# x times W1_r of 44 node blocks computed ahead, kept in HBM, and loaded in place of x

## The chip, the core and the metric

The kernel runs on one core of a Trainium2 chip. A core has five engines with queues of their own: TensorE (PE, matrix products into PSUM; PEld is its weight load), VectorE (DVE), ScalarE (ACT), GpSimd (POOL, which here issues the indirect loads that gather rows) and SyncE (SP, which here issues nearly all other transfers). Each engine works off its instructions in order and waits on semaphores for the others. The metric is the device time of one execution in microseconds (us), lower is better. Three executions of the kernel before took 3142.34, 3150.2 and 3154.97 us; the median is 3150.2 us.

## What is computed

Two graph convolutions, a linear layer, a residual and a layer norm, over 12500 nodes of 256 features and 200000 edges sorted by destination:

```python
def _sage_conv(x, src, dst, W_l, b_l, W_r):
    msgs = x[src]
    agg = segment_sum(msgs, dst, num_segments=N_NODES)
    deg = segment_sum(ones, dst, num_segments=N_NODES)
    mean = agg / maximum(deg, 1.0)[:, None]
    return mean @ W_l + b_l + x @ W_r
h = relu(_sage_conv(x, src, dst, W1_l, b1, W1_r))
h = relu(_sage_conv(h, src, dst, W2_l, b2, W2_r))
out = layernorm(x + h @ W3 + b3)
```

The destinations are crowded at low node numbers. All numbers are fp32.

## The kernel before

Nodes are cut into 98 blocks (`NB`) of 128. The sums over edges are made in two ways, and both run beside each other through each of the two layers.

Blocks 0 to 11 (six groups of 256 nodes in the first layer, `HG1 = 6`, `DN = 256`) have so many edges that a dense count matrix is cheaper: `count` (L887) builds, tile by tile of 128 edges, the number of edges from every source to every destination of the group. DVE makes 0/1 masks (`pick` L912, `low` and `aft` L902), PE multiplies them into `count_ps` (L946, L950), and ACT writes them to SBUF (L952). `product` (L820) then multiplies the counts with x, split in three bf16 parts (L842), block by block, and `degrees` (L964) sums the counts (L970). The next group is counted while the last one is multiplied.

All other blocks are gathered. A round (`Gathers.step`) is four indirect loads of 128 rows each on POOL (L277) into one of four buffers `got`, and eight small PE products (L289, `part_ps`); every one or two rounds, further products (L305, L311) put the sums in order, and DVE adds them to a ring `sums` (L315, L319). The first layer has 257 rounds. A round's buffer is free for the gather of four rounds later once its L289 products have run.

When a block's sums are complete, `first_block` (L1127) makes its layer output in three pieces: it loads the block's x (`load_rows`, L1067) and yields; it turns x by two PE transposes (L1073) and an ACT copy (L1075) and yields; `sage` (L1098) multiplies turned x by W1_r (two L1102 products, which show as four rows) and the sums by W1_l (L1104), DVE adds the bias (L1111) and the scaled sums (L1112), ACT takes the maximum with 0 (L1157), and SP stores the block (L1160, L1163).

PE and POOL are in an order written out by the program itself. `layer` (L627) takes one round after another, with up to three pieces of waiting blocks, and then fills the round with pieces of the dense work (count, product, degrees, given by `stages_1`) until the largest of its cost sums over PE, DVE and ACT reaches 5.05. When the dense work is used up, a round is only gathers and block pieces. In the last 8 rounds the dense work must be done; then come the rest of the blocks. Stage 0 of `stages_1` counts the first group with no product beside it; its count begins after the setup.

The setup (L321 to L581) loads the edge lists and turns them into tables: `columns` (L398) is a ping-pong of DVE, which makes a column of keys (L517), PE, which transposes it (L404), and DVE, which clamps it into a table (L407). Twelve gather rounds (`early_round`, L476) stand between. At its end DVE runs tests on the edge lists (L531 to L579) that decide at the very end of the program whether a second method has to run (it does not here). The memory pools of the counts are opened after the setup's pool closes and lie on its memory.

Of the kernel before, what the change touches and what calls it, by code (L numbers as in the profile page):

```python
# [25 lines left out]
P = 128  # L26
# [23 lines left out]
def by_runs(  # L50
# [66 lines left out]
    def room(t):  # L117
        return ROOMS[t // 32]
# [15 lines left out]
    h2_d = dram.tile([P, NB, 2, D], F32, name="h2_d")  # L134
    ORDER = [*reversed(range(HG1)), *range(HG1, HG)]
# [106 lines left out]

    def left_after(g):

        return NB if g == len(groups) - 1 else min(max(int(at_least(groups[g + 1][0]) // P), 0), NB)
# [75 lines left out]
    with tc.tile_pool(name="setup", bufs=1) as su, \  # L321
            tc.tile_pool(name="setup_ps", bufs=2, space=PSUM) as su_ps:
# [159 lines left out]


# [8 lines left out]
        columns(low, (0, HC), low_t, "low", 0, 0, HT)  # L492
        high = su.tile([P, HC, P], F32, name="high")
# [14 lines left out]
        for g in ORDER:  # L508
# [6 lines left out]
            for i, (to, name, since) in enumerate(((key_t[g], "key", lows[g]), (after_t[g], "aft", after_from[g]))):  # L515
# [3 lines left out]
                columns(key, (c0, c1), to, name, c0, since, highs[g])  # L519

# [5 lines left out]

        early_round()
# [8 lines left out]
                                       op1=OP.mult, accum_out=test())  # L536
        early_round()
# [39 lines left out]
        for a, b in zip([FIRST - 1] + ends, ends):  # L577
# [3 lines left out]
                                       accum_out=test(1))  # L581


    def weight(w, name, tag, queue=nc.scalar):
        t = consts.tile([P, NC, w.shape[1]], F32, name=name, tag=tag)
        queue.dma_start(t, w.rearrange("(c p) f -> p c f", p=P))
        return t

    w1l_sb, w1r_sb = weight(w1l, "w1l_sb", "wl"), weight(w1r, "w1r_sb", "wr")
# [17 lines left out]
    def held(g):  # L607

        return counts[ORDER.index(g) % 2]

# [487 lines left out]
    def sage(own_t, b, agg, since, wl, wr, bias):  # L1098

        ps = block_bank()  # L1100
        for c in range(NC):
            nc.tensor.matmul(ps[:, 1], lhsT=own_t[:, c], rhs=wr[:, c], start=c == 0, stop=c == NC - 1)  # L1102
# [8 lines left out]
        nc.vector.tensor_add(own, ps[:, 1], bias)  # L1111
# [15 lines left out]
    def first_block(b, agg=None):  # L1127
        x_sb = load_rows(x, N, b, "x_sb")
# [16 lines left out]
        ps = turned()  # L1145
        known = of_ring and b in upto
        if known:
            summed(ps)
        x_t = transposed(x_sb, ps, "own_t")
        yield 0.5, 0.0, 0.37  # L1150
# [5 lines left out]
        h = sage(x_t, b, agg, since, w1l_sb, w1r_sb, biases[:, 0])  # L1156
# [7 lines left out]
        yield 1.75, 1.65, 1.1  # L1164
# [430 lines left out]
```

## Time and profile before

| what | us |
|---|---|
| median of 3 runs (lowest, highest) | 3150.2 (3142.34, 3154.97) |
| the profiled execution, its own time | 3149.7 |
| its span on the core's trace | 3147.4 |
| setup, to the first count product | 0 to 97 |
| stage 0 (first count) | 97 to 205 |
| rest of the first layer | 205 to 1688 |
| second layer | 1688 to 3147 |

Busy time and "x" counts are per engine; "PEclk" is the share of the full TensorE clock that the throttle granted. A row of the chain of waits is a start, a length, and the instruction (engine, tile, line, number of rows) that the end of the program hung on in that time. "remote" or "another core or an unknown queue" stands where a semaphore came without an instruction that the trace could name for it; this program runs on one core.

### The profile page before, as it was taken

Reading aid. Unit: us, or ns where it says so; the run is one execution under the profiler, and the core shown is the slowest. Engines: PE = TensorE matmul, PEld = TensorE weight load, DVE = VectorE, ACT = ScalarE, POOL = GpSimd, SP = SyncE. Lnnn points to the kernel's source line nnn. Section 1 sums busy time; section 2 is a strip of 40 time slices with the busy share of each in tenths; the row PEclk is TensorE's granted clock in tenths of the full one; section 3 lists DMA queues with packets and bytes.
Section 4 is the critical chain, followed back from the end, with each engine's and each line's share of the span. In section 5 each row is a group of like instructions: output and inputs, shape, how many; then the busy total and the mean of one; then the engine's idle time right before and its main releaser. Section 6 shows DMA issues by size and latency. Waiting matters only on the chain.

```text
span 3147.4 us, 51161 instructions
## 1 busy us (share of the span) xinstructions
PE 2509.2 (80%) x17028; PEld 1731.9 (55%) x17028; DVE 1422.9 (45%) x4363; ACT 1345.2 (43%) x2435; POOL 1887.7 (60%) x1946
## 2 busy tenths in 40 slices
PE   3578888888888888888876878887877888887876
PEld 1245556566655555556653555555655556665654
DVE  5566644344444476654232124334543344343344
ACT  0476644445455411463122444555554445433322
POOL 6666756556566566665654665666655666666653
PEclk8799989899899898999987998999989899998989
DMA  4359887786776555656755876777767777676643
GB/s 118 87 181 316 275 266 230 221 267 217 242 243 207 160 176 176 186 168 203 251 160 176 266 236 209 253 243 223 234 217 225 229 227 234 209 223 193 203 139 93
DMA packets 392876, 659.49 MB, mean 210 GB/s; under 512 B 61055, under 2 KB 217757, under 8 KB 392605
## 3 DMA queue, kind: packets, MB, share of 16 engines
q1 hardware_dynamic: 295315, 401.44, 40.0%
q0 software_dynamic: 92928, 253.88, 26.5%
q8 instruction: 140, 2.29, 0.3%
q10 hardware_dynamic: 4362, 0.80, 0.2%
q14 instruction: 131, 1.07, 0.1%
HBM read 559.60 MB, written 96.29 MB: 208 GB/s over the span
## 4 chain that ended last, share of the span: by engine, by line
PE 69%; issue 9%; DVE 6%; ACT 5%; another core or an unknown queue 5%; DMA 3%; POOL 0%; DVEq 0%; ACTq 0%; SPq 0%; POOLq 0%
PE dense_ps L842 11%; PE part_ps L289 9%; PE count_ps L946 9%; PE dense_ps L877 6%; PE beside_ps L877 6%; PE block_ps L1102 5%; PE block_ps L1104 5%; PE sum_ps L305 5%; PE block_ps L1185 3%; ACT counts L952 3%; PE block_ps L1073 3%; PE count_ps L950 2%; DMA x_in<-in_x_dram 1%; PE dense_ps L873 1%
## 5 line engine op out<-in xcount | busy, mean ns | idle before, releaser
L277 POOL DMA_INDIRECT got<-in_x_dram,src_t x1028 | 1017.9, 990 | 642.7 <-issue 248.6
L277 POOL DMA_INDIRECT got<-h_d,src_t x908 | 867.6, 955 | 584.1 <-issue 226.1
L952 ACT CAST counts<-count_ps 128x882 f32 (+3 forms) x744 | 681.2, 916 | 436.9 <-PE count_ps L946 130.4
L946 PE MATMUL count_ps<-pick,low 128*128 128x490 bf16 (+2 forms) x1300 | 429.6, 372 | 220.6 <-ACT counts L952 100.4
L842 PE MATMUL dense_ps<-counts,rows 128*128 128x256 bf16 x3528 | 504.0, 282 | 33.3 <-issue 16.4
L912 DVE TENSOR_SCALAR pick<-steps,tables 128x686 bf16<-128x686 f16 (+3 forms) x872 | 361.0, 421 | 319.3 <-PE count_ps L946 110.3
L842 PEld LDWEIGHTS <-rows 128*128 128x128 bf16 x3528 | 340.7, 101 | 147.2 <-issue 67.8
L877 PE MATMUL dense_ps<-wide,rows 128*128 128x512 f32 x784 | 354.9, 453 | 32.9 <-issue 13.1
L289 PE MATMUL part_ps<-got,one 128*32 128x257 f32 (+1 forms) x3872 | 338.2, 416 | 30.2 <-DMA got<-h_d,src_t 11.1
L299 ACT COPY some<-part_ps 128x257 f32<-128x257 f32 (+1 forms) x345 | 128.7, 373 | 518.1 <-PE part_ps L289 197.2
L877 PE MATMUL beside_ps<-wide,rows 128*128 128x512 f32 x784 | 325.2, 415 | 0.2 <-issue 0.2
L233 DVE TENSOR_TENSOR one<-lo_t,lane_b 128x128 f32<-128x128 bf16 x484 | 139.1, 288 | 380.8 <-PE part_ps L289 111.0
L319 DVE TENSOR_TENSOR sums<-sums,sum_ps 128x256 f32 x345 | 141.8, 411 | 269.7 <-PE beside_ps L877 62.3
L305 PE MATMUL sum_ps<-two,some 128*128 128x128 f32 x1380 | 232.2, 292 | 32.9 <-ACT some L299 15.4
L789 ACT CAST wide<-counts 128x512 fp32r<-128x512 bf16 x245 | 148.2, 619 | 244.1 <-PE beside_ps L877 99.4
L305 PEld LDWEIGHTS sum_ps<-two,some 128*128 128x128 f32 x1380 | 208.0, 204 | 70.2 <-ACT some L299 26.7
L950 PEld LDWEIGHTS <-low 128*128 128x128 bf16 x736 | 86.8, 118 | 258.7 <-issue 250.1
L946 PEld LDWEIGHTS <-low 128*128 128x128 bf16 x1300 | 147.2, 116 | 130.9 <-issue 56.3
L877 PEld LDWEIGHTS dense_ps<-wide,rows 128*128 128x128 f32 x784 | 160.9, 205 | 91.5 <-issue 37.6
L1111 DVE TENSOR_TENSOR own<-block_ps,biases 128x256 f32<-128x256 f32 x196 | 82.6, 422 | 238.2 <-PE block_ps L1104 88.5
L950 PE MATMUL count_ps<-aft,low 128*128 128x98 bf16 x736 | 188.2, 256 | 0.0
L877 PEld LDWEIGHTS beside_ps<-wide,rows 128*128 128x128 f32 x784 | 159.7, 204 | 29.7 <-issue 0.6
(200 smaller groups left out, 3024.9 us busy)
## 6 DMA issues: line engine op xcount, KB each, us to landing
rows<-h_d SPq DMA_DIRECT2D x490, 256.0 KB
rows<-x_d SPq DMA_DIRECT2D x245, 384.0 KB
h_d<-split SPq DMA_DIRECT2D x98, 256.0 KB
count_d<-counts SPq DMA_DIRECT2D x28, 896.0 KB
spare<-count_d SPq DMA_DIRECT2D x157, 128.0 KB
x_d<-rows SPq DMA_DIRECT2D x49, 384.0 KB
got<-in_x_dram,src_t POOLq DMA_INDIRECT x1028
got<-h_d,src_t POOLq DMA_INDIRECT x908
```

Of the source, the lines that this page charges most:

```text
L277: rows = nc.gpsimd.indirect_dma_start(out=g[:, j, :D], out_offset=None, in_=self.table, in_offset=bass.IndirectOffsetOnAxis(ap=src_t[:, e: ...
L289: strip = nc.tensor.matmul(part_ps[j * W:(j + 1) * W, :width], lhsT=one[:, j], rhs=g[:, j, :width], start=r == 0, stop=r == n - 1)
L305: nc.tensor.matmul(sum_ps[:, c], lhsT=some[:, c * P:(c + 1) * P], rhs=two, start=True, stop=True)
L789: nc.scalar.copy(wide.bitcast(F32R), counted)
L842: nc.tensor.matmul(ps[:, c], lhsT=rows[:, b % 2, k, c * P:(c + 1) * P], rhs=c_sb[:, b, :DN], start=False, stop=b == NB - 1 and k == 2 and ...
L877: nc.tensor.matmul(ps[c], lhsT=own[:, k, c * P:(c + 1) * P].bitcast(F32R), rhs=of.bitcast(F32R), start=u + k == 0, stop=u == NB - 1 and k ...
L912: nc.vector.tensor_scalar(r[:, :w * NB], steps[:, :w * NB], key_t[g][:, t - lo_g:t - lo_g + 1], None, op0=OP.is_equal)
L946: nc.tensor.matmul(c[:, a * NB:b * NB], lhsT=s, rhs=r[:, a * NB:b * NB], start=True, stop=alone)
L950: nc.tensor.matmul(c[:, :NB], lhsT=before[0], rhs=before[1], start=False, stop=True)
L952: nc.scalar.copy(to[:, :, bass.ds(off_act.at(t), w)], c.rearrange("p (d s) -> p s d", s=NB))
L1102: nc.tensor.matmul(ps[:, 1], lhsT=own_t[:, c], rhs=wr[:, c], start=c == 0, stop=c == NC - 1)
L1104: product = nc.tensor.matmul(ps[:, 0], lhsT=agg[:, c], rhs=wl[:, c], start=c == 0, stop=c == NC - 1)
```

## The change

The product of x and W1_r needs nothing of the edges. For blocks 12 to 55 (`OWNED`, the first 44 gathered ones) it is made ahead by a new generator, `own_parts`, and stored in a new HBM array `own_d`; `first_block` loads the block's row from `own_d` instead of x, does no transposes and no W1_r products, and adds the loaded row to the bias. 29 blocks are made in the setup, a step at a time between its other PE instructions, with ACT copies, six rooms in the setup's pool and two PSUM banks of their own. The other 15 are a part beside the first count (stage 0), with DVE copies. A step is two transposes of one block and the two products of the block before. A block costs one load of 128 KB from x, one store and one load of 128 KB of `own_d`, where it cost one load of x.

```diff
+    OWNED = range(HG1 * DN // P, HG1 * DN // P + 44)
+    own_d = dram.tile([NB * P, D], F32, name="own_d")
...
+    def own_parts(blocks, room, bank, copy, since=None):
+        rooms, last = {}, None
+        while blocks or last is not None:
+            for b in blocks[:3]:
+                if b not in rooms:
+                    rooms[b] = room()
+                    load = nc.sync.dma_start(rooms[b][:, 0], x[b * P:(b + 1) * P, :])
+                    if since is not None and b < OWNED[0] + 3:
+                        tc.add_manual_dep(load.ins, since, LANDED, reason="the gathers' tables first")
+            b = blocks.pop(0) if blocks else None
+            if b is not None:
+                t, ps = rooms[b], bank()
+                for c in range(NC):
+                    nc.tensor.transpose(ps[:, 0, c * P:(c + 1) * P], t[:, 0, c * P:(c + 1) * P], ident)
+                copy(t[:, 1], ps[:, 0])
+                rooms[b] = t, ps
+            if last is not None:
+                t, ps = rooms.pop(last)
+                for c in range(NC):
+                    nc.tensor.matmul(ps[:, 1], lhsT=t[:, 1, c * P:(c + 1) * P], rhs=w1r_sb[:, c],
+                                     start=c == 0, stop=c == NC - 1)
+                copy(t[:, 0], ps[:, 1])
+                nc.sync.dma_start(own_d[last * P:(last + 1) * P, :], t[:, 0])
+            last = b
+            yield 1.25, 0.85, 0.0
...
         early_round()
+        w1l_sb, w1r_sb = weight(w1l, "w1l_sb", "wl"), weight(w1r, "w1r_sb", "wr")
+        still_own = list(OWNED)
+        now_own = still_own[:29]
+        del still_own[:29]
...
+        owning = own_parts(now_own, own_room, own_bank, nc.scalar.copy, strips[0])
+        def owned(n=1):
+            for _ in range(n):
+                next(owning, None)
+        owned(3)
...
         columns(low, (0, HC), low_t, "low", 0, 0, HT)
+        owned()
...
                 columns(key, (c0, c1), to, name, c0, since, highs[g])
+                owned()
...
+        owned(2)
         early_round()
...
+        owned(2)
         early_round()
...
+        owned(len(now_own) + 1)
...
+    def still_owned():
+        ps = dense_pool.tile([P, 2, 256], F32, name="own_ps", tag="dense_ps")
+        def room():
+            return rows_pool.tile([P, 3, D], F32, name="own_room", tag="rows", bufs=N0)
+        return own_parts(still_own, room, lambda: ps, nc.vector.tensor_copy), 1.25 * len(still_own)
...
+            if k == 0:
+                parts.append(still_owned())
...
-        for c in range(NC):
+        for c in range(NC if own_in is None else 0):
             nc.tensor.matmul(ps[:, 1], lhsT=own_t[:, c], rhs=wr[:, c], start=c == 0, stop=c == NC - 1)
...
-        nc.vector.tensor_add(own, ps[:, 1], bias)
+        nc.vector.tensor_add(own, ps[:, 1] if own_in is None else own_in, bias)
...
-        x_sb = load_rows(x, N, b, "x_sb")
+        own_in = load_rows(own_d, NB * P, b, "x_sb") if b in OWNED else None
+        x_sb = load_rows(x, N, b, "x_sb") if own_in is None else None
...
-        x_t = transposed(x_sb, ps, "own_t")
-        yield 0.5, 0.0, 0.37
+        x_t = transposed(x_sb, ps, "own_t") if own_in is None else None
+        yield (0.5, 0.0, 0.37) if own_in is None else (0.1, 0.0, 0.0)
...
-        yield 1.75, 1.65, 1.1
+        yield 1.75 if own_in is None else 0.88, 1.65, 1.1
```

The two weight loads stay on ACT's queue and only stand earlier in the program. In the order of the built program, the number of PE products, transposes and weight loads is the same before and after; ACT has 14 copies more (58 new, 44 fewer of L1075), DVE 30 copies more, SP 88 transfers more, POOL none.

More of the change, by code (lines that the diff above doesn't have):

```diff
@@ L1155, in first_block @@
             degree(ps)
-        h = sage(x_t, b, agg, since, w1l_sb, w1r_sb, biases[:, 0])
+        h = sage(x_t, b, agg, since, w1l_sb, w1r_sb, biases[:, 0], own_in)
         nc.scalar.activation(h, h, AF.Relu)
```

18 lines of the change are left out of this document (11 added, 7 removed).

## The prediction

> **What bounds the kernel now.** I read the page's totals first, then its chain of waits by engine, then the same engine counts cut into the kernel's stages.
>
> ```profile
> span 3147.4 us, 51161 instructions
> PE 2509.2 (80%) x17028; PEld 1731.9 (55%) x17028; DVE 1422.9 (45%) x4363; ACT 1345.2 (43%) x2435; POOL 1887.7 (60%) x1946
> PE 69%; issue 9%; DVE 6%; ACT 5%; another core or an unknown queue 5%; DMA 3%; POOL 0%; DVEq 0%; ACTq 0%; SPq 0%; POOLq 0%
> ```
>
> PE holds 69% of the chain. That is a mean over stages, so here is the view by stretches. Its columns are the stretch and its length, then busy time and instructions of PE, PEld, DVE, ACT and POOL, the granted clock, the DMA share and GB/s.
>
> ```profile
> 27.00:97.00 70.00, 25.68 (x164) 12.72 (x164) 43.72 (x166) 2.25 (x6) 49.34 (x46) 0.74 0.29 86
> 97.00:205.00 108.00, 71.24 (x402) 36.24 (x403) 57.31 (x167) 73.47 (x87) 67.80 (x68) 0.82 0.34 99
> 205.00:460.00 255.00, 208.81 (x1665) 137.82 (x1664) 153.82 (x397) 156.34 (x253) 164.26 (x155) 0.91 0.88 282
> 460.00:1200.00 740.00, 623.33 (x5104) 437.45 (x5103) 355.96 (x1142) 317.77 (x537) 446.80 (x466) 0.92 0.70 221
> 1500.00:1602.00 102.00, 86.82 (x694) 62.56 (x691) 33.81 (x118) 17.08 (x52) 62.54 (x67) 0.97 0.74 239
> 1602.00:1688.00 86.00, 59.26 (x439) 40.33 (x439) 35.27 (x123) 21.08 (x58) 31.84 (x33) 0.80 0.47 147
> 1640.00:1660.00 20.00, 14.29 (x81) 9.08 (x77) 11.23 (x38) 7.68 (x21) 13.36 (x14) 0.91 0.64 202
> ```
>
> From 205 to 1602 PE is busy 82 to 85% of the time. In the setup from 27 on it is busy 37%, with POOL and DVE above it; in stage 0 it is busy 66%, and ACT (68%) leads. So the change moves PE work out of a stretch that PE sets into two that it doesn't. Layer 2 (1688 to 3147) has the same instructions in both programs and is taken at no change.
>
> **The removed work.**
>
> ```profile
> L1102 PE MATMUL block_ps<-w1r_sb,own_t 128*128 128x256 f32 x392 | 117.1, 426 | 5.8 <-ACT own_t L1075 1.9 <-PE part_ps L289 1.0 <-issue 0.9
> L1073 PE MATMUL block_ps<-ident,x_sb 128*128 128x128 f32 x196 | 45.1, 314 | 1.3 <-PE part_ps L289 1.3
> ```
>
> Busy time over 98 blocks is 117.1 / 98 = 1.19 and 45.1 / 98 = 0.46: 1.65 us a block, 73 us for 44. But this does not come off the time. Rounds are filled up to 5.05 whatever the blocks need, so a block that gets cheaper lets in dense work earlier. The layer's length is its 257 rounds, and a round can't be shorter than its four gathers:
>
> ```profile
> L277 POOL DMA_INDIRECT got<-in_x_dram,src_t x1028 | 1017.9, 990 | 642.7 <-issue 248.6
> 69.00 0.95 POOL L277 DMA_INDIRECT got<-in_x_dram,src_t  x1 [0.30 <-issue]
> ```
>
> The built order of the two programs gives what is left: the last dense product L842 stands in round 245 before and in round 232 after, so 13 rounds turn from filled into light ones. (The costs in the code say nearly the same: 44 x (0.40 + 0.87) = 56 is 11 budgets of 5.05.) A filled round took 740 / 466 x 4 = 6.35 us from 460 to 1200, and 6.09 from 1500 to 1602. A light one costs at least 4 x (0.99 + 0.30) = 5.16; from 1640 to 1660, with no dense work but many blocks, it was 20 / 14 x 4 = 5.71. I take the middle, 5.43: 13 x (6.35 - 5.43) = **-12**, with ends at -4 (0.3 a round, if the 6.09 hold and the light ones are as slow as 5.71) and -16.
>
> **The tail** (1602 to 1688). Dense blocks 0 and 1 wait in it before; after, their last pieces come earlier, and only block 91 is left from the queue. The chain's rows for a block, at full clock and at the lower one, and for the degrees that still filled rounds there:
>
> ```profile
> 1609.16 1.29 PE dense_ps L970 x43
> 1611.71 1.21 PE dense_ps L970 x42
> ...
> 1670.23 1.06 PE block_ps L1102 x4
> 1671.29 0.86 PE block_ps L1104 x4
> ...
> 1674.36 0.37 PE block_ps L1073 x2
> ...
> 1677.82 1.71 PE block_ps L1102 x4
> 1679.53 1.72 PE block_ps L1104 x4
> ```
>
> A block is 0.37 + 1.06 + 0.86 = 2.3, or 0.74 + 1.71 + 1.72 = 4.2 at the low clock. Two blocks are 4.6 to 8.4, I take 6; the degrees, whose last round goes from 248 to 234, add 2 of these 2.5. Together **-8**. The ends are -2 (gathers cover both) and -15 (both at the low clock, the degrees, and 4 us of waits between blocks).
>
> **The setup.** 29 steps are added to PE's order, at most three together save at its end. PE is busy 25.68 of 70 from 27 on. At 1.65 a step that makes 25.68 + 47.9 = 73.5, so 3.5 more than there is. What lies in this stretch already:
>
> ```profile
> 59.19 16.07 another core or an unknown queue
> ...
> 60.00:70.00 10.00, 0.00 (x0) 0.00 (x0) 0.00 (x0) 0.00 (x0) 7.57 (x8) 0.50 0.35 105
> 40.00:50.00 10.00, 7.40 (x58) 3.56 (x56) 8.66 (x40) 0.75 (x2) 6.84 (x6) 1.00 0.26 78
> 90.00:100.00 10.00, 3.76 (x16) 1.25 (x17) 10.00 (x34) 1.95 (x2) 8.42 (x6) 0.50 0.24 69
> ```
>
> In 16 us of it all engines but POOL stood still for a PE event that the trace can't explain. If more PE work shifts or ends this stall, the steps are free; if it comes again, they have 54 us. At 0.37 + 1.06 = 1.43 a step, without waits, the sum is 25.68 + 41.5 = 67.2, and nothing is added. DVE's tests (L531 to L579) that end the setup now can go between the key steps, since the next keys wait for PE longer.
>
> New waits: SP alternates a store of `own_d` and the load for the room that it frees, and that load stands behind the landing.
>
> ```profile
> 1638.00 1.55 DMA h_d<-own
> ...
> 1685.27 2.01 DMA h_d<-own
> ...
> 205.04 2.79 DMA x_pair<-in_x_dram
> ...
> L1075 ACT ACTIVATE own_t<-block_ps 128x256 f32<-128x256 f32 x196 | 75.3, 384 | 114.8 <-PE block_ps L1073 62.7 <-PE block_ps L1185 13.8 <-PE count_ps L946 9.0
> ```
>
> Store and issue make some 2.4 us; 23 such pairs (29 less six rooms) make 55, within the 70, so SP keeps up with one step in 2.4 us, but hardly faster. Behind a late room load stands PE's own transpose, and behind that the key transposes (L404), for which DVE waits. The first three room loads wait for the first gather round, so PE, whose own transposes stand ahead of the products for `after` (L458), is held some 2 us there. And the memory of the counts lies on the rooms: the first picks, low weights and counts copy of stage 0 wait until the last store has landed, 0.4 for ACT's copy (as L1075) and 2.0. I add 3.5 for PE and 2.4 for this store: **+6**. The low end is 0; the high end +36, all 29 steps at the low clock (0.74 + 2.04; 2.04 is the row below), 25.68 + 80.6 = 106.3.
>
> ```profile
> 1632.79 2.04 PE block_ps L1102 x4
> ```
>
> [...]
>
> **Stage 0.** 15 steps, about one in each of rounds 12 to 26; the stage keeps these rounds in both programs.
>
> ```profile
> L952 ACT CAST counts<-count_ps 128x882 f32 x68 | 68.6, 1009 | 27.1 <-DVE pick L912 10.4 <-remote 8.4 <-PE count_ps L946 3.4
> 110.43 7.00 another core or an unknown queue
> 121.08 4.81 another core or an unknown queue
> L1111 DVE TENSOR_TENSOR own<-block_ps,biases 128x256 f32<-128x256 f32 x196 | 82.6, 422 | 238.2 <-PE block_ps L1104 88.5 <-remote 56.4 <-issue 56.0
> ```
>
> PE gains 15 x 1.65 = 25, to 96 of 108; DVE two copies of some 0.42 (as L1111) a step, 12.6, to 70; ACT, with 73.5, still leads less the 44 copies that it loses. That is cover for the work but not for its order: DVE's first three bias adds are moved up behind the first picks and wait for a load of `own_d` queued on SP behind the last store (1 to 2 us), and the `x_pair` loads of stage 1 need rooms that the last own stores free (2.79 already on the chain there). I take **+3**: one such wait and a copy or two in the way of picks. The ends are +8 (PE at the low clock: 15 x 2.5 = 37, 108 of 108, both waits), and -10 (stalls of 7.0 and 4.8 gone). The 88 added transfers are 128 KB each, 11.5 MB, two thirds of it in stretches with a DMA share of 0.29 and 0.34: nothing is added for bytes.
>
> **The sum** against the profiled execution, 3149.7: 3149.7 + 6 + 3 - 12 - 8 = **3139**. This execution is 0.5 below the median of the runs, so the forecast for the median is 3139 too.
>
> **The rivals.**
>
> *The setup and stage 0 take the steps for nothing* (3124). PE's steps fall into the 16 us stall and run warm, light rounds reach the gathers' floor (-14), the tail gives -12: 3149.7 - 26. For it: the idle 44 us of PE in the setup, and a clock of 1.00 where it is busy. Against: the setup's chain runs DVE to PE to DVE, so every step that comes between a key and its transpose shows.
>
> *The setup becomes PE's* (3170), on the slow side. Place: PE's order between the key transposes. Price: steps at the low clock, 2.45 (0.74 + 1.71) to 2.78 each, 25.68 + 71 to 81, so +27 to +36, and the last store 2.4: +34; stage 0 +6; less 20 in the layer: 3149.7 + 20. It decides from a step of 44.3 / 29 = 1.53 us upwards, and outweighs the gain from 1.53 + 20 / 29 = 2.2 us. For it: clock 0.74 in the mean and 0.50 at the end of the setup. Against: the 1.00 from 40 to 50. SP's 2.4 us a pair would give the same sign but only if PE waits for rooms throughout.
>
> *The work goes but the light rounds are no shorter* (3155). Gathers or the buffers' release hold a round near 6: 13 x 0.3 = -4, tail -2, setup +8, stage 0 +3: 3149.7 + 5. For it: 6.09 and 5.71 in two stretches with less beside the gathers. Against: 0.30 between back-to-back gathers while PE was silent.
>
> **How the numbers follow.** The forecast gets 0.45, the free setup 0.27, PE's setup 0.15, the unshortened rounds 0.13. The likeliest case's own range is 3128 to 3153 (+6 to 0 or +14, the light rounds by 4 and the tail by 6 either way, not all at one end). The range 3112 to 3168 takes in the free setup down to one stage 0 stall less, and leaves out half of PE's setup and a little below. A measurement of this kernel tells about 0.5% (15.7 us) from no change: below 3134.5 is faster, above 3166 slower. Faster: 0.25 of the free setup and 0.13 of the forecast, 0.38. Slower: most of PE's setup, the ends of the others, 0.15. Within: 0.47.
>
> **What would show it.** After: the first L946 near 103 (97 means the setup was free, above 115 that PE or SP sets it); the granted clock from 27 to 97 (above 0.9: warm steps); PE's idle time ahead of `own_room` transposes, named SP or DMA, if rooms are late; the second L946 group's start, the stage's end near 214; the last L842 some 13 rounds before its place now, with gathers 1.29 to 1.43 us apart behind it; the stretch from there to the end of the layer with two blocks fewer. The prediction is wrong if filled rounds change their 6.35, if the unexplained stalls grow or vanish (16, 7 and 5 us here, as large as the result), or if layer 2 moves.

## The result and the profile after

The changed kernel took 3175.09 us in the median of 8 runs (3166.72 to 3183.3), the kernel before 3152.18 (3142.34 to 3160.08). The ratio is 1.0071, with a 95% interval from 1.005 to 1.0093: slower by some 22 us, where 3139 was forecast with a range up to 3168. A gain was forecast, and it came out as a loss.

The page of the changed kernel, its totals and its chain by engine:

```profile
span 3174.0 us, 51493 instructions
PE 2514.4 (79%) x17028; PEld 1730.2 (55%) x17028; DVE 1429.9 (45%) x4393; ACT 1355.9 (43%) x2449; POOL 1904.0 (60%) x1946
PE 64%; issue 9%; DVE 5%; ACT 4%; another core or an unknown queue 4%; DMA 4%; ACTq 0%; DVEq 0%; SPq 0%; POOL 0%; POOLq 0%
```

PE's instructions are the same 17028 and its busy time is nearly the same (2509.2 before). The change moved work of PE; it saved next to none. The view by stretches of the changed kernel, with the stretches set to its own stages (columns as in the prediction):

```profile
27.00:124.00 97.00, 68.12 (x348) 43.25 (x347) 46.37 (x175) 23.47 (x64) 61.35 (x57) 0.84 0.56 167
124.00:224.00 100.00, 77.05 (x456) 44.87 (x456) 67.14 (x192) 73.77 (x85) 55.05 (x57) 0.95 0.43 126
224.00:1550.00 1326.00, 1095.98 (x8906) 751.12 (x8905) 692.25 (x2124) 590.04 (x1003) 820.73 (x819) 0.91 0.72 229
1550.00:1637.00 87.00, 58.92 (x480) 41.36 (x479) 31.23 (x110) 17.94 (x52) 53.28 (x56) 0.73 0.48 143
1637.00:1710.00 73.00, 49.99 (x246) 31.51 (x246) 31.99 (x112) 17.63 (x51) 31.37 (x32) 0.79 0.50 151
```

The setup now ends at 124 instead of 97, and in it PE is busy 68 of 97 us at a clock of 0.84, so it is neither at 1.00 nor at 0.50 throughout (0.50 is what 60 to 70 of the kernel before showed, with PE idle). Its busy time is what the prediction had summed up (67.2 at 1.43 a step); but 97 us went by for it, and not 70. Stage 0 is shorter (99 instead of 107). The fourth row holds the light rounds: PE is 68% busy, at 0.73 of its clock. The last row, the tail from round 249 on, is 73 instead of 86.

To compare runs by stage I take five places out of each trace: the start of the first count product (the setup), the end of the 68th copy of counts (stage 0), the start of round 249, the first gather of layer 2 (the tail lies between these two), and the end. The runs fell on different chips, and the kernel before is much faster on some: 3117 to 3152 us on chips of the first kind, 2623 to 2625 on those of the second. No chip was seen in both; whether it is the chip itself or something else at the time of the runs that makes the kind is not known. All comparisons below are within a kind. The columns are lengths in us, from one profile each; a ratio is of the medians of several runs:

| run | setup | stage 0 | rest to round 249 | tail | layer 2 | ratio to before (95%) |
|---|---|---|---|---|---|---|
| first kind: before | 97.0 | 107.1 | 1398.5 | 85.6 | 1459.2 | |
| before_third | 95.9 | 107.3 | 1384.6 | 89.3 | 1434.9 | |
| changed | 124.2 | 99.2 | 1413.8 | 73.3 | 1463.5 | 1.0071 (1.005 to 1.0093) |
| after_third | 128.1 | 103.6 | 1389.0 | 76.4 | 1456.2 | one run |
| warm | 127.6 | 103.4 | 1389.0 | 77.7 | 1439.9 | 1.0091 (1.0059 to 1.0122) |
| act_rooms | 123.7 | 104.9 | 1379.7 | 77.3 | 1438.0 | one run |
| first_out | 127.3 | 99.5 | 1380.0 | 72.1 | 1446.5 | one run |
| split15 | 125.8 | 91.5 | 1390.3 | 70.9 | 1434.0 | 1.0012 (0.9984 to 1.0039) |
| only15_again | 93.1 | 114.9 | 1404.3 | 78.4 | 1440.0 | 1.0101 (1.0052 to 1.0151) |
| best33 | 104.0 | 101.8 | 1387.3 | 70.8 | 1462.5 | 0.9974 (0.9945 to 1.0003) |
| best33_again | 100.4 | 107.4 | 1397.2 | 75.2 | 1455.8 | 0.9995 (0.9965 to 1.0024) |
| key18_again | 106.8 | 96.2 | 1390.0 | 80.6 | 1447.0 | 1.0007 (0.998 to 1.0033) |
| second kind: before_again | 90.7 | 88.7 | 1150.2 | 69.5 | 1215.1 | |
| after_again | 118.5 | 96.3 | 1165.9 | 58.8 | 1230.8 | 1.0138 (1.0112 to 1.0165) |
| old_cost | 119.0 | 99.5 | 1144.8 | 71.0 | 1217.4 | 1.0118 (1.0061 to 1.0176) |
| only29 | 113.4 | 84.6 | 1157.8 | 56.3 | 1216.7 | 1.0069 (1.0046 to 1.0092) |
| act_store | 105.8 | 99.4 | 1161.4 | 59.9 | 1217.5 | 1.008 (1.0052 to 1.0107) |
| rooms12 | 103.4 | 102.8 | 1163.7 | 59.6 | 1221.9 | one run |
| only15 | 91.0 | 102.6 | 1158.4 | 69.8 | 1218.3 | 1.0057 (1.003 to 1.0085) |
| key18 | 92.3 | 84.5 | 1152.7 | 66.5 | 1221.7 | 0.9979 (0.996 to 0.9998) |

Layer 2 has the same instructions in all rows. It shows how much one profile says: 1434 to 1464 on the first kind, so "rest" and "layer 2" are good to some 15 us there. The setup is not so blurred: 93 to 97 on the first kind without steps in it, 124 to 128 with 29.

### The profile page after: what moved, and what is told of

The parts are those of the page before. It is cut to its first block, busy times and chain, and to the rows that moved or that the text cites. A ratio compares the mean times of both kernels' runs of the same rounds, so it can differ in the third digit from the quotient of the medians.

```text
span 3174.0 us, 51493 instructions
## 1 busy us (share of the span) xinstructions
PE 2514.4 (79%) x17028; PEld 1730.2 (55%) x17028; DVE 1429.9 (45%) x4393; ACT 1355.9 (43%) x2449; POOL 1904.0 (60%) x1946
## 4 chain that ended last, share of the span: by engine, by line
PE 64%; issue 9%; DVE 5%; ACT 4%; another core or an unknown queue 4%; DMA 4%; ACTq 0%; DVEq 0%; SPq 0%; POOL 0%; POOLq 0%
PE dense_ps L894 10%; PE count_ps L998 8%; PE part_ps L323 8%; PE dense_ps L929 6%; PE beside_ps L929 6%; PE block_ps L1166 5%; PE sum_ps L339 5%; PE block_ps L1164 4%; PE block_ps L1248 4%; PE block_ps L1135 3%; ACT counts L1004 2%; PE count_ps L1002 2%; DMA x_in<-in_x_dram 2%; DMA rows<-h_d 1%
## 5 line engine op out<-in xcount | busy, mean ns | idle before, releaser
L311 POOL DMA_INDIRECT got<-in_x_dram,src_t x1028 | 1032.3, 1004 | 651.3 <-issue 248.6
L311 POOL DMA_INDIRECT got<-h_d,src_t x908 | 869.5, 958 | 585.2 <-issue 228.0
L1004 ACT CAST counts<-count_ps 128x882 f32 (+3 forms) x744 | 681.9, 917 | 400.4 <-PE count_ps L998 163.1
L998 PE MATMUL count_ps<-pick,low 128*128 128x490 bf16 (+2 forms) x1300 | 423.9, 369 | 201.3 <-ACT counts L1004 99.2
L964 DVE TENSOR_SCALAR pick<-steps,tables 128x686 bf16<-128x686 f16 (+3 forms) x872 | 360.0, 420 | 274.0 <-PE count_ps L998 113.2
L323 PE MATMUL part_ps<-got,one 128*32 128x257 f32 (+1 forms) x3872 | 335.4, 411 | 20.6 <-DMA got<-h_d,src_t 11.6
L998 PEld LDWEIGHTS <-low 128*128 128x128 bf16 x1300 | 146.9, 115 | 128.4 <-issue 57.7
L1248 PE MATMUL block_ps<-split,h_t 128*128 128x256 f32 x392 | 121.2, 436 | 55.9 <-ACT h_t L1137 20.4
```

Of the source, the lines that this page charges most:

```text
L311: rows = nc.gpsimd.indirect_dma_start(out=g[:, j, :D], out_offset=None, in_=self.table, in_offset=bass.IndirectOffsetOnAxis(ap=src_t[:, e: ...
L323: strip = nc.tensor.matmul(part_ps[j * W:(j + 1) * W, :width], lhsT=one[:, j], rhs=g[:, j, :width], start=r == 0, stop=r == n - 1)
L964: nc.vector.tensor_scalar(r[:, :w * NB], steps[:, :w * NB], key_t[g][:, t - lo_g:t - lo_g + 1], None, op0=OP.is_equal)
L998: nc.tensor.matmul(c[:, a * NB:b * NB], lhsT=s, rhs=r[:, a * NB:b * NB], start=True, stop=alone)
L1004: nc.scalar.copy(to[:, :, bass.ds(off_act.at(t), w)], c.rearrange("p (d s) -> p s d", s=NB))
L1248: nc.tensor.matmul(y[:, 0], lhsT=h2_t[:, c], rhs=w3_sb[:, c], start=c == 0, stop=c == NC - 1)
```

## The experiments

Lines of the changed kernel that the rows name: in `own_parts` the load L257, the transposes L264, their copy L265, the products L270, their copy L272, the store L273; the gather is L311, part products L323, count product L998 and its copy L1004, picks L964, a block's load L1129 and products L1164 and L1166.

**Where the 22 us arise: the setup or stage 0.** Two kernels, each with one half of the change (the first edit keeps the 15 blocks beside the first count, the second the 29 of the setup):

```diff
-    OWNED = range(HG1 * DN // P, HG1 * DN // P + 44)
+    OWNED = range(HG1 * DN // P, HG1 * DN // P + 15)
-        now_own = still_own[:29]
-        del still_own[:29]
+        now_own = still_own[:0]
+        del still_own[:0]
```

> 15 blocks instead of 44, none made in the setup, all 15 beside the first count. Theory: the setup's 29 steps cost the 27 us (first count product at 124.2 instead of 97.0) and stage 0 bears its 15 steps for nothing (99 us with them, 107 without), so the first count begins near 97 again, stage 0 takes 97 to 108, and the time comes to within 10 us of before, 3140 to 3155. Rival: the steps of stage 0 cost too, hidden in the changed kernel by fewer stalls: stage 0 above 112, time 3160 or more.

```diff
-    OWNED = range(HG1 * DN // P, HG1 * DN // P + 44)
+    OWNED = range(HG1 * DN // P, HG1 * DN // P + 29)
...
-            if k == 0:
+            if k == 0 and still_own:
```

> 29 blocks instead of 44, all made in the setup, none beside the first count. Theory: the setup ends as late as in the changed kernel, first count product 120 to 126; the rounds give nothing back, the time is 3165 to 3178. Rival (the steps beside the first count are what costs): stage 0 gets shorter than 99 us, the time falls below 3160.

The times in both expectations were written for the first kind of chip and can't be compared; the stages can. Without steps in the setup it ends at 91.0, as before (90.7); with 29 it ends 23 later. But stage 0 isn't free: 102.6 with the 15 steps against 84.6 without them and 88.7 before. Both halves cost, and their ratios, 1.0057 and 1.0069, add up to nearly that of the whole change on this kind, 1.0138. What stands behind stage 0's cost is a row of the view of waits of only15 in stage 0 (engine and tile, what it waited for: us in total, times, longest):

```profile
PEld own_ps L270 <- DVE own_room L265: 14.0, 13, 2.3
```

In stage 0 both halves of a step use one PSUM bank (in the setup two banks take turns, and no wait of L270 for L265 is among the largest there). The products stand right behind the transposes in PE's order and wait until DVE has copied these, and that copy stands behind picks in DVE's. 13 waits, 14.0 us.

> 15 blocks beside the first count and none in the setup, once more. Theory: no delay in the setup (first count product within 4 of before), so the ratio is below 1.007, the changed kernel's, wherever it runs; by the steps' waits for DVE's copy stage 0 is 0 to 14 longer than before's. Rival: the setup isn't the cost, ratio again 1.007 or more.

The second run of the 15 blocks, on the first kind of chip, had the setup at 93.1 but a ratio of 1.0101, above the theory's bound of 1.007, though the interval (from 1.0052) still holds this bound. Stage 0 is 7.6 above before_third, and the rest 20 above, more than the 15 by which a single profile is uncertain there. What made the rest longer was not found. Its waits for L265 in stage 0 were 23.3 us, one of them 10.7.

**The same kernels once more under the second conditions,** as the base of the other rows:

> The kernel before once more, for a second profile under the conditions of the runs above, which take some 2620 us where the first ones took 3150. Theory: its rounds last 5.1 to 5.3 us as in the changed kernels there, so a filled round is already at the length of its gathers and the light rounds can't gain; the first count product comes at 82 to 92, and stage 0 lasts 84 to 90 as without its 15 steps. Rival: the kernel before has a stall in its setup each time; first count product at 97 or later.

> The changed kernel once more under these conditions. From the four variants: setup 113 to 119 to the first count product (25 to 30 more than before), stage 0 some 99 to 102 (15 more), the rest of layer 1 by 10 to 14 less, all of it in the tail behind round 249 (57 to 60 instead of 70); ratio to before 1.008 to 1.012. Rival: the ratio stays at 1.005 or less because the light rounds give 12 back, as predicted.

Setup +27.8, stage 0 +7.6, tail -10.7. The rest of the layer did not get shorter; it is 15.7 longer in this pair. But layer 2, with the same instructions, is 15.7 longer too in this profile, which was taken in the slowest of the four runs (2672.81, the median is 2662.66), so these 15.7 can't be put down to the change. The time is 1.4% above before, more than expected. The rounds there last 5.0 to 5.2 in both kernels: from round 235 to 249 5.03 before and 5.04 after. There was nothing left for a light round to win. These are the gathers of the kernel before, from 400 to 1000 on the second kind and from 460 to 1200 on the first, in the view of groups (busy, mean ns, idle before and what ended it):

```profile
L277 POOL DMA_INDIRECT got<-in_x_dram,src_t x470 | 456.1, 970 | 144.8 <-issue 120.7 <-DMA got<-in_x_dram,src_t 7.8 <-PE count_ps L946 4.9
```

```profile
L277 POOL DMA_INDIRECT got<-in_x_dram,src_t x468 | 449.8, 961 | 290.5 <-issue 110.8 <-PE part_ps L289 60.7 <-PE count_ps L946 33.8
```

The first row is of before_again, the second of before_third. Nearly the same number of gathers, and nearly the same length of one. On the second kind POOL hardly waits (144.8 over 470 is the 0.31 between two gathers); on the first it waits for PE.

> The kernel before, one profile under this call's conditions. If its time is near 3120 to 3150: first count product 85 to 100, stage 0 100 to 110, rounds 6.2 to 6.4; if near 2620: 90.7, 88.7 and 5.1, as in the profile already taken. Either is what the two next runs are read against.

> The changed kernel, one profile under this call's conditions. Theory: setup 25 to 32 longer than the profile beside it, stage 0 within 10 of it, tail 8 to 14 shorter, and nothing won in the light rounds. Rival: the setup's 27 of the first profile was a chance of one execution, under 15 here.

On the first kind the pair repeats the first profiles: setup +32.2, stage 0 -3.7, tail -12.9. The setup's delay was no chance.

Where in the setup it arises is seen at the last table of keys, the last write of `afters` (the kernel before first, then changed and after_third):

```profile
82.70 0.20 DVE L407 TENSOR_SCALAR afters<-aft_ps 128x56 bf16<-128x56 f32 x1
97.92 0.22 DVE L442 TENSOR_SCALAR afters<-aft_ps 128x56 bf16<-128x56 f32 x1 [0.89 <-issue]
102.82 0.21 DVE L442 TENSOR_SCALAR afters<-aft_ps 128x56 bf16<-128x56 f32 x1 [3.62 <-PE own_ps L264]
```

It stands at 80.48 in before_third. So the last table comes 15 and 22 later, and from it to the first count product it is 26 and 25 us instead of 14 and 15. More than half of the delay arises ahead of the last table, with the three steps ahead of the products for `after` and those beside the keys.

Stage 0 is shorter on the first kind although its 15 steps wait there too. In the kernel before it holds these waits for events without a name (view of waits of stage 0):

```profile
DVE pick L912 <- remote: 12.3, 3, 6.8
ACT counts L952 <- remote: 8.4, 4, 3.9
```

In stage 0 of the changed kernel, after_third and split15 that view has none; on the second kind the stage got longer (96.3 against 88.7).

**What holds the setup.** SP's queue in the changed kernel shows a load of a room and a store in turn (start, length of the issue, operation):

```profile
98.20 0.33 SPq L257 DMA_DIRECT2D own_room<-in_x_dram  x1
98.58 0.42 SPq L273 DMA_DIRECT2D own_d<-own_room  x1
101.65 0.33 SPq L257 DMA_DIRECT2D own_room<-in_x_dram  x1
102.03 0.42 SPq L273 DMA_DIRECT2D own_d<-own_room  x1
104.12 0.33 SPq L257 DMA_DIRECT2D own_room<-in_x_dram  x1
104.50 0.42 SPq L273 DMA_DIRECT2D own_d<-own_room  x1
107.60 0.33 SPq L257 DMA_DIRECT2D own_room<-in_x_dram  x1
```

Each load stands 2.1 to 3.1 behind the store ahead of it, the pair takes 3.1 in the mean here ((107.60 - 98.20) / 3), and the next store is issued at once behind the load, so it had been held up by it. Two kernels take that away in two ways: stores from ACT's queue, or 12 rooms.

```diff
-                nc.sync.dma_start(own_d[last * P:(last + 1) * P, :], t[:, 0])
+                store.dma_start(own_d[last * P:(last + 1) * P, :], t[:, 0])
...
-        owning = own_parts(now_own, own_room, own_bank, nc.scalar.copy, strips[0])
+        owning = own_parts(now_own, own_room, own_bank, nc.scalar.copy, strips[0], nc.scalar)
```

> The setup's stores of own_d are issued on ACT's queue instead of SP's, nothing else. Theory: SP's pair of a store and a room load, each load behind the landing of the store just issued (some 3.0 us a pair in the trace), sets the setup from 47 to 111; without it the first count product comes at 103 to 112 and the time falls by 12 to 21, to 3154 to 3163. Rival: PE's own work between the key steps sets the setup, the first count product stays at 118 to 126 and the time at 3170 to 3180.

```diff
-            return su.tile([P, 2, D], F32, name="own_room", bufs=6)
+            return su.tile([P, 2, D], F32, name="own_room", bufs=12)
```

> 12 rooms instead of 6 for the setup's steps, the stores on SP as in the changed kernel. Theory: SP's pairs of store and load set the setup; with 17 pairs instead of 23 to wait for, the first count product comes 8 to 15 earlier than in the changed kernel beside it. Rival: PE's work sets it; no more than 3 earlier.

On the second kind both did as the theory said: the setup ends at 105.8 and 103.4, against 113.4 to 119.0 in the three kernels with six rooms and SP's stores. The waits of PE in the setup, of after_again first and of rooms12 second:

```profile
PE own_ps L264 <- DMA own_room<-in_x_dram: 17.5, 11, 3.7
```

```profile
PE own_ps L264 <- DMA own_room<-in_x_dram: 1.6, 1, 1.6
```

11 of the steps waited for their room, 17.5 us; with 12 rooms one did. That is 8 to 16 us, a third to a half of what the setup lost on this kind; the other part stays. On the first kind PE hardly waits for rooms: in the changed kernel's own profile there is one such wait in the setup, 4.9 us, though SP's queue shows the pairs above. Both cures at once, and the first three steps put to the end:

> Both at once: 12 rooms, and the setup's stores on ACT's queue. Theory: 12 rooms and the other queue mend the same wait, so the first count product comes at 101 to 106, as with either alone; what is left against before (90 to 91) is PE's steps between key transposes and the last steps. Rival: the two waits are separate, and it comes below 97.

```diff
-        owned(3)
```

> Stores on ACT's queue, and the first three steps are no longer ahead of the products for after; the 29 blocks are the same, so three more steps come at the end of the setup. Theory: what is left of the setup's delay is the number of steps at its end, PE's work (1.43 a step), not the place of the first three: first count product within 3 of the 105.8 with the stores alone. Rival: the wait of these three for their rooms (5 in the changed kernel's profile) is carried to the end; 5 to 8 earlier.

These two fell on the first kind of chip, for which their numbers had not been written, and missed them. Against 124.2 to 128.1 of the changed kernel there, 123.7 and 127.3 say that neither SP's pair (act_rooms) nor the place of the first steps (first_out) is worth more than some 4 us on it. So SP's pair does not explain the delay there. What a step waits for there is seen in act_rooms, in a part of its timeline (start, length; in brackets the idle time ahead and what ended it):

```profile
70.52 1.03 PE L270 MATMUL own_ps<-w1r_sb,own_room 128*128 128x256 f32 x4
...
79.76 0.37 ACT L272 COPY own_room<-own_ps 128x256 f32<-128x256 f32 x1 [4.53 <-remote]
...
80.19 0.69 PE L264 MATMUL own_ps<-ident,own_room 128*128 128x128 f32 x2 [8.42 <-issue]
```

By the records PE's four rows end at 71.55. ACT, after 4.53 us of idleness for which the trace names no instruction, copies them only at 79.76, and PE's next step, which needs that bank, starts at 80.19. As the records have it, the products' event reached ACT 8 us late. The profile models the ends of products, so these may have run late themselves; which of the two it was, and why, is open. A step is a round trip from PE to ACT and back, and to SP and HBM for its room, and each is exposed to this: in the setup of after_third PE's transposes waited 12.2 us for the copy that frees their bank, 10.7 of it at one time. The end of the setup shows steps with hardly any other work beside them (changed kernel; the first row is the last table once more):

```profile
97.92 0.22 DVE L442 TENSOR_SCALAR afters<-aft_ps 128x56 bf16<-128x56 f32 x1 [0.89 <-issue]
98.12 0.44 PE L264 MATMUL own_ps<-ident,own_room 128*128 128x128 f32 x2 [0.24 <-ACT own_room L272]
...
102.71 0.44 PE L264 MATMUL own_ps<-ident,own_room 128*128 128x128 f32 x2 [1.47 <-ACT own_room L272]
...
111.06 0.69 PE L264 MATMUL own_ps<-ident,own_room 128*128 128x128 f32 x2 [4.46 <-issue]
...
123.13 0.45 DVE L964 TENSOR_SCALAR pick<-steps,tables 128x882 bf16<-128x882 f16 x1 [1.41 <-DMA own_d<-own_room]
```

At 97.92 DVE makes the last table, and in the kernel before it would go on to its tests. Here these had been done between the key steps. Eight steps and a last product are left, and with the products of the last gather rounds they take 25 us, some 3 a step, where PE is busy 16.4 of the 25; and the first pick waits for the last store, as expected.

**Steps that hurt less.** 18 steps, one beside each key step, none ahead of the products for `after` and none at the end; stores from ACT's queue:

```diff
-    OWNED = range(HG1 * DN // P, HG1 * DN // P + 44)
+    OWNED = range(HG1 * DN // P, HG1 * DN // P + 18)
-        owned(3)
```

> 18 blocks, one beside each key step of the setup, stores on ACT's queue, no steps ahead of the products for after, none at the end of the setup, none beside the first count. Theory: what is left is 18 steps of 1.45 between key transposes, partly under DVE's work: first count product 3 to 15 later than before; stage 0 as before; the tail 4 to 10 shorter; ratio 0.996 to 1.004. Rival: any step between key transposes costs its full length, 26 and more; ratio above 1.006.

On the second kind the setup ends at 92.3, 1.6 later than before; the ratio is 0.9979, and its interval just leaves out 1. The steps are nearly free there because something else moved: the last table came 12.5 later than in before_again (81.50 instead of 69.0), but DVE's tests were done by then, and only 11 us stood behind it instead of 22. With 29 steps and the same store queue (act_store) the setup ended 13.5 later than with these 18 (on another chip of this kind), so the eleven steps ahead of the products for `after` and behind the last key cost some 1.2 each, most of their work of 1.43. Then the step of stage 0 in two pieces, so that other work stands between the transposes and the products:

```diff
+                if since is None and last is not None:
+                    yield 0.4, 0.42, 0.0
             if last is not None:
...
-            yield 1.25, 0.85, 0.0
+            yield (1.25, 0.85, 0.0) if since is not None else (0.85, 0.43, 0.0)
```

> The changed kernel with the step beside the first count cut in two pieces: the transposes of a block, and, after other pieces of the round, the products of the block before. Theory: with one PSUM bank the products stand right behind the transposes and wait for DVE's copy of these, which stands behind picks (some 1 us a step, 12 to 18 in the stage); cut in two, the copy is done by then: stage 0 at 84 to 90 instead of 96 to 103, the time 8 to 15 less than the changed kernel's 1.0138, so a ratio of 1.007 to 1.011. Rival: the stage is longer because PE and DVE have the work itself to do; stage 0 at 95 or more.

Stage 0 took 91.5, just above the expected 84 to 90 (which was written for the second kind), against 99.2 to 104.9 in the five profiles on the first kind with 15 whole steps after a setup of 29. The wait is gone: the weight loads of the own products waited 8.5 us in ten times for DVE's copy in after_third (first row), and in split15 the two waits of such a load (L272 in its numbering) are for other DVE instructions, the longer of them in the second row:

```profile
PEld own_ps L270 <- DVE own_room L265: 8.5, 10, 0.9
```

```profile
PEld own_ps L272 <- DVE sums L355: 1.7, 1, 1.7
```

The ratio is 1.0012, its interval from 0.9984 to 1.0039 lies below the changed kernel's. So this one edit takes back most of the loss. How much of that is stage 0 is less sure, since its gain of 8 to 13 in the profile is about half of it. The setup was still at 125.8 in this kernel, so a setup 30 us longer can be made up for elsewhere (here by stage 0, -16, and the tail, -18, against before_third). Both together:

> 33 blocks: 18 beside the key steps with stores on ACT's queue, as in the run of 18 (ratio 0.998), and 15 beside the first count with the step cut in two. Theory: setup 92 to 94, stage 0 at 84 to 90, and the tail 5 to 10 shorter than with 18: ratio 0.992 to 0.998. Rival: the steps beside the first count still cost 10 or more; ratio 1.000 to 1.005.

> 33 blocks once more (18 beside the key steps, 15 beside the first count in two pieces). Theory: where rounds last 5.1, setup +2, stage 0 as before or 4 less, tail 10 less than before: ratio 0.993 to 0.998; where they last 6.3, setup +8, stage 0 -5, tail -15: 0.994 to 1.000. Rival: the gain of the first run was chance, ratio 1.000 to 1.004.

> 18 blocks once more, none beside the first count. Theory: less of the tail is won than with 33 (66.5 against 56 to 60 in the profiles where rounds last 5.1), so it is 2 to 8 us slower than the 33 on the same chip: ratio 0.996 to 1.001. Rival: the 15 steps beside the first count cost as much as they win; both ratios within 0.001.

33 blocks gave 0.9974 and then 0.9995, both intervals hold 1; 18 blocks gave 1.0007 on the chip of the second of these. On the first kind of chip the setup is 3 to 11 longer with 18 steps, the tail 10 to 18 (33 blocks) or 5 to 9 (18 blocks) shorter. The two ratios on one chip differ by 0.0012, 4 us, with intervals that overlap. No version was found that surely beats the kernel before on the first kind. In these two runs stage 0 with split steps took 101.8 and 107.4, with stalls of 4.7 and 8.8 us by events without a name, so its 91.5 is no sure value either.

**The light rounds.** Is it the planner's cheaper cost for a loaded block that brings nothing?

```diff
-        yield (0.5, 0.0, 0.37) if own_in is None else (0.1, 0.0, 0.0)
+        yield 0.5, 0.0, 0.37
...
-        yield 1.75 if own_in is None else 0.88, 1.65, 1.1
+        yield 1.75, 1.65, 1.1
```

> The costs that first_block gives to the planner stay those of before for all blocks, so the dense work is spread over as many rounds as before. Theory: rounds last what PE really has to do in them, so the filled rounds get shorter where blocks are loaded instead of made (44 blocks of 1.65 us, some 0.2 to 0.3 a round), there are few light rounds, and the time falls by 10 to 40 to 3135 to 3165. Rival (as in the prediction): a filled round lasts 6.4 whatever its blocks need; then the rounds stay as long, the two blocks come back to the tail, and the time is 3175 to 3190.

With the old costs the dense work is used up as late as before, and the tail is as long as before (71.0 against 69.5; 58.8 with the new costs). The rest is 1144.8, 5 less than before and 17 to 21 less than in the other kernels of 44 blocks. So the new costs are what shortens the tail, and by these single profiles they give it all back on the way there; the ratio, 1.0118, can't be told from the 1.0138 with the new costs. The theory that filled rounds would get shorter by 0.2 to 0.3 was wrong where rounds are at the length of their gathers already.

On the first kind the light rounds are no shorter either: 6.26 and 6.10 from round 235 to 249 in the changed kernel, 6.14 and 6.01 before. What fills them is in the chain of waits of the changed kernel:

```profile
1578.91 3.36 another core or an unknown queue
...
1583.04 2.05 PE block_ps L1164 x4
1585.09 1.71 PE block_ps L1166 x4
...
1591.84 3.04 another core or an unknown queue
...
1618.44 6.69 another core or an unknown queue
```

A block's products take 2.05 and 1.71 us there, with a granted clock of 0.50 from 1583 to 1587, against 1.06 and 0.86 with a clock of 1.00 in the kernel before (1670 to 1672.2); and events without a name make 13 us in three places. The theory, a guess, was that PE has the low clock for want of work, so I gave it some:

```diff
+    def warmed():
+        ps = dense_pool.tile([P, 2, 256], F32, name="warm_ps", tag="dense_ps")
+        nc.tensor.matmul(ps[:, 0], lhsT=ident, rhs=w1r_sb[:, 0], start=True, stop=True)
...
                 fill(whole * (part + 1) / 3, part == 0)
+                if over and n_pieces == 3 and i + 1 < n - left:
+                    warmed()
```

> The changed kernel with 39 more PE products of 128x256, three in each of its 13 light rounds, whose results nobody reads. Theory (where rounds last 6.2 to 6.4): a light round is no shorter than a filled one because PE, with gaps, runs at 0.77 of its clock and its events come late; with more for PE to do the clock in these rounds rises above 0.9 and they last 5.3 to 5.8 instead of 6.25, 5 to 12 us less between round 235 and 249. Where rounds last 5.1 anyhow (gathers back to back): no change, 5.0 to 5.2. Rival: the light rounds are held by the gathers themselves; 39 x 0.38 = 15 us of PE work more, and the rounds stay at 6.2 or get longer.

Rounds 235 to 249 in the view by stretches of before_third, after_third and warm:

```profile
1503.00:1587.00 84.00, 72.79 (x584) 52.12 (x584) 28.94 (x101) 15.41 (x46) 52.40 (x56) 0.96 0.72 234
```

```profile
1535.00:1620.00 85.00, 58.45 (x488) 39.76 (x487) 32.08 (x114) 19.29 (x56) 53.58 (x56) 0.76 0.49 145
```

```profile
1525.00:1620.00 95.00, 76.98 (x548) 53.20 (x548) 33.19 (x114) 19.29 (x54) 53.01 (x57) 0.77 0.44 133
```

The theory fell. With 39 products more in the light rounds, most of them in this stretch, the clock stayed at 0.77 and the rounds got longer, 6.76 instead of 6.10. So a light round on this chip isn't held by its gathers (more PE work makes it longer), and these products did not raise the clock (0.76 in after_third, 0.77 in warm). From before_third to after_third PE's busy time in these rounds fell by 14 us (72.79 to 58.45), and its idle time rose by as much (11.2 to 26.6), so nothing was won. Why the idle time came, the events without a name apart, and what would bring the clock up was not found.

## Why the prediction was wrong

- *What bounds the kernel, and what is moved:* right. PE holds the chain, and the 1.65 us a block left the layer: the last dense product stands 13 rounds earlier (at 1545.8 instead of 1597.7), as the built order said.
- *The setup, +6:* the step that failed most. It measured +27 and +32. The price of a step was right: PE's busy time from 27 on came to 68.12 and 66.60, where 67.2 was summed. What failed is the next step, that these 67.2 fit into the 70 us that were there, "and nothing is added", with "I add 3.5 for PE and 2.4 for this store" as the rest. The 44 us in which PE was idle were no room: they are waits in a chain between engines, and most of the steps' time came on top of them: PE was still idle for 29 of the 97 us. The last table came 15 and 22 later. DVE's tests did move between the key steps, as predicted, but the steps left for the end took 25, more than the 14 that stood behind the last table before. SP's pair was priced at 2.4 from two landings of stores and judged to keep up; it takes about 3, and on the second kind PE waited for rooms (17.5 us in after_again; 8 to 16 us were won back there). On the first kind, for which the forecast was made, it explains some 4 us at most (act_rooms, one profile). What holds each step there, its own trip over ACT, the two banks or the late events, was not separated, and a kernel with more banks was not run.
- *Stage 0, +3:* -8 and -4 on the first kind, within the range given, +8 on the second. The wait that costs there was not seen: DVE's copy between transposes and products that share a bank. With the step cut in two the ratio was 1.0012 instead of 1.0071. That the stage got shorter on the first kind all the same is luck: it had waits for events without a name before, 20 us in the two rows above, and none in the changed kernel, after_third and split15. The prediction named that as the low end of its range; why they went is open. PE's "to 96 of 108" was too much (76 and 82 in the two profiles), and by that sum PE, not ACT with 73.5, would have led the stage, other than the prediction has it.
- *The light rounds, -12:* nothing. The step that failed is "I take the middle, 5.43": both ends were rows of other work, and the 5.71 came from a stretch of 20 us. The rival of unshortened rounds, with 0.13, was the one that held, by its number: its 6.09 was the right row (6.26 and 6.10 in the light rounds). Of its two reasons the first, the gathers, did not hold on the first kind (with more PE work the rounds got longer); the second, the release of the buffers, which waits for PE, was not tested by itself.
- *The tail, -8:* -12.3 and -12.9; direction and reason right (old_cost gives it back), the size a third too small.
- *The case that came nearest* is the rival that the setup becomes PE's (3170, chance 0.15), by its price of +34 and not by its mechanism: the clock in the setup was 0.84, and of its steps most took 0.44 + 1.03 (17 of 29 product pairs took the 1.03), as at 98.12, where the clock was 1.00 from 98 to 100.

In sum, forecast +6 +3 -12 -8 = -11; the two pairs on the first kind give in the mean setup +30, stage 0 -6, rest +10, tail -13, so +21 before layer 2, with the ratio's +22 beside it. Of these, the +10 lies within what one profile can tell. The added steps brought the setup's clock from 0.74 to 0.84 (from 0.71 to 0.86 between before_third and after_third), and they were not free for that.

## What to carry to other kernels

PE's idle time in a chain between engines was no room for work here: the busy times fitted (68 of 70 us), and the setup still ended 27 and 32 us later. See what the chain does at the place where a step goes in, and not only whether the busy times fit. Steps were cheap where other work could move under them (18 beside the keys: 1.6 us in all on the second kind, 3 to 11 on the first), and dear where nothing was left to cover them (some 3 us each at the end of the setup, for 1.43 of work). When two halves of a step share a PSUM bank, put other work of the same engine between them: the weight loads of the second half waited 8.5 us for the copy in stage 0 of after_third, and had no wait for it among the largest in split15. A round that has lost its filler is only worth what its next bound leaves (6.26 and 6.10 us here on the first kind, where 5.43 was forecast): look for that bound in a stretch of the same work before taking a middle.

## What the runs showed of the hardware

The same program takes 2623 to 2625 us on some chips and 3117 to 3152 on others. The length of a gather is nearly the same (970 and 961 ns in the rows above); what differs is POOL's idle time ahead of some 470 gathers, 144.8 and 290.5, and the granted clock, 0.968 and 0.910 in before_again and before_third. In the chain of waits from 600 to 1000, events without a name have 7.4% in before_third and are not among the ten largest shares in before_again. On the first kind a wait for PE products ended 8 us after the products did by the records (the row of act_rooms), and in the setup of the kernel before one wait of PE ends after 16.7 us by an event without a name; of DVE's waits from 55 to 95 in before_again none ends by such an event, and the longest is 9.42 us, for products of PE. What makes them late was not found. A change whose worth lies in PE's time has to be judged on both: in the kernel before, a round was 6.0 to 6.4 us on the one kind (from 460 on) and 5.0 to 5.2 on the other (from 400 on), close to the bare length of its gathers (4 x (0.97 + 0.31) = 5.1).
